# Layer 1 of a two-layer CIN on one Trainium2 core: double batches of leftover products, spread loads, and another order at the beginning

## The chip, the cores and the metric

The kernel runs on one core of one Trainium2 chip. The metric is the device time of one execution in microseconds (us); of several executions the median is taken. The engines are named as the profile names them: PE is TensorE (PEld its weight loads), DVE is VectorE, ACT is ScalarE, POOL is GpSimd, SP is SyncE, whose queue issues most DMAs. A main matmul in fp32 shows as two records in the trace.

## The reference

`x` has 4096 rows, 32 fields and 16 embedding values, in fp32. Two layers of pairwise products follow each other, and their results are summed over the embedding:

```python
def _cin_layer(out, x, W, b, gamma, beta):
    r, _, e = x.shape
    h = jnp.einsum('rne,rfe->rnfe', out, x).reshape(r, -1, e)
    h = jnp.einsum('rce,oc->roe', h, W) + b[None, :, None]
    return _batchnorm(h, gamma, beta)          # over rows and embedding
h1 = _cin_layer(x, x, W1, b1, g1, beta1)       # 32*32 products -> 128 channels
out, direct1 = (h1[:, :64], h1[:, 64:])
direct2 = _cin_layer(out, x, W2, b2, g2, beta2)  # 64*32 products -> 128 channels
agg = jnp.concatenate([direct1, direct2], axis=1)
return agg.sum(axis=-1)
```

Both batchnorms take their mean and variance over all 65536 sites (a site is one row and one embedding value).

## The kernel before

Channels lie on partitions and sites on the free axis, in 128 tiles of 512 sites (`NT`, `T`). The products of layer 1 are symmetric in the two fields, so the two halves of `W1` are added (on POOL, L312), and each pair of fields is multiplied once. For a tile, 512 of the pairs are four blocks of 128 rows: DVE multiplies `a` by `b` (512 KB each, loaded by `load_main` on SP's queue, four buffers each) into `z` in one instruction (L387), and PE does four matmuls of 128 rows into one PSUM bank `ps` (L428). The 16 pairs that are left (fields 16 apart) would fill only 32 partitions with padding, so `r` packs those of eight tiles: 2 groups of 16 rows in each of four row groups. DVE multiplies them into `zr` once in eight tiles (L373), and `add_leftovers` (L380) does four matmuls of 32 rows, each in another row group of the array and for another tile's bank. This is called a batch here. It is issued once in four tiles, ahead of the main matmuls of the tiles that it starts; for tiles 0 to 3 it is issued after tile 1, and it ends the sums of tiles 0 and 1.

The main loop runs over tiles 0 to 123 (L428 in its body). At each turn it issues the loads of the next tile, the product `z`, a batch where one is due, the four main matmuls and `finish(t - 1)`: the eviction of the tile before. An eviction is three activations on ACT (`e` with all channels for the statistics, `kept` for layer 2, `ed` for the direct sum: L352, L355, L358), `bn_stats` on DVE (L115), and for each second tile a store of `kept` and a reduction over the embedding on DVE (L364). PSUM has 8 banks: six in `psum` (tag `ps`) and two in `factors` (tag `f`), which layer 1 does not use but for warming up (`begun`, `BEGIN` matmuls of ones at the start, L239) and for a small product at its end.

Each engine runs its own instructions in the order in which the program names them, but for hints `tc.issue_after`. So what stands ahead of a waiting `z` on DVE, or of a load on SP's queue, is set by where it is written in the loop. `zpool` has four buffers; the second half of the weights (`w1m_sb`) uses one of them at the start. At turn 20 the weights of layer 2 are combined on DVE (`combine_weights`), at turns 12 and 14 two selection matrices are reduced (`spread`, `block`). The list `EARLY` spreads work for layer 2 over the turns: differences of fields of odd tiles (`load_x` into `xs`, `negate`, `difference`, `store_difference`, four times in 24 turns each), and the first operands of layer 2 (`load_b`, `load_bx`, `load_a`).

The last four tiles (124 to 127) are done by halves of the output channels (L461), kept channels first, so that the batchnorm of layer 1 is known while the other halves run. Layer 2 takes 64 steps `c` of two tiles, with four stages `k` each, by a scheme in the manner of Strassen: DVE makes products `zz`, POOL sums of them `t` (L703, L714), PE does the matmuls (L698) in column halves of 64 outputs, two at a time. The products of a stage are issued in four parts, `x2`, `x54` of the stage before (which has waited for POOL), `x31` and `x67`.

At the start SP's queue issues tile 0 in four parts of 256 KB, then `a`, `b` of tile 1, the first `r`, and so on; ACT's queue issues the two halves of the weights of layer 1 (384 KB each) and the batchnorm vectors. The first two tiles' products are made in chunks of 512 columns (`multiply_chunk`, L396).

Of the kernel before, what the change touches and what calls it, by code (L numbers as in the profile page):

```python
# [61 lines left out]
BEGIN = 3  # L63
# [7 lines left out]
def tile_cin(ctx: ExitStack, tc: tile.TileContext, xa, xb, xr, w1, w1m, w2, bn, out):  # L71
# [20 lines left out]

    nc.scalar.activation(const.tile([P, 1], FP, tag="sd", name="table"), eps, AF.Sqrt)
# [93 lines left out]
    def load_x(g, k):  # L187

        at = xb.offset + ((2 * DIFF * g + 1) * WRAP + 2 * k) * T
        nc.sync.dma_start(xs[:, k], bass.AP(xb.tensor, at, [[2 * WRAP * T, DIFF], [4 * T, 8], [1, 2 * T]]))  # L190
# [15 lines left out]
    for g in range(NC // DIFF):  # L206
        at = 14 + 24 * g
        EARLY += [(at + 2 * k, lambda g=g, k=k: load_x(g, k)) for k in range(2)]
        EARLY += [(at + 12 + 2 * k, lambda k=k: negate(k)) for k in range(2)]
        EARLY += [(at + 16 + 2 * k, lambda k=k: difference(k)) for k in range(4)]  # L210
        EARLY += [(at + 23, lambda g=g: store_difference(g))]
    early = []
    EARLY += [(75, lambda: early.append(load_b(0))), (83, lambda: early.append(load_bx(0)))]
    EARLY += [(91 + 8 * k, lambda i=i: early.append(load_a(0, i))) for k, i in enumerate(STAGES)]
# [48 lines left out]
    with ExitStack() as one:  # L263
        lpool = one.enter_context(tc.tile_pool(name="lpool", bufs=4))
# [7 lines left out]
        xs = xpool.tile([P, 2, 2 * T], FP, tag="x", name="xs")  # L272
# [9 lines left out]
        def load_main(t):  # L282
            a = lpool.tile([P, 2 * T], FP, tag="a", name="a")
            b = lpool.tile([P, 2 * T], FP, tag="b", name="b")

            def load(to, part, n):
                at = part * T
                if to is a:
                    at += xa.offset + t * FIELDS * 2 * T
                    source = bass.AP(xa.tensor, at, [[2 * T, FIELDS], [0, 4], [1, n * T]])  # L290
                else:
                    at += xb.offset + (t * WRAP + 2) * T
                    source = bass.AP(xb.tensor, at, [[T, FIELDS], [4 * T, 4], [1, n * T]])
                return nc.sync.dma_start(to[:, part * T : (part + n) * T], source)

            if t == 0:

                parts = ((a, 0, 1), (b, 0, 1), (b, 1, 1), (a, 1, 1))
            else:
                parts = ((a, 0, 2), (b, 0, 2))  # L300
            for part in parts:
                last = load(*part)
            loads.append(last)
            return a, b

        w1_sb = wpool.tile([P, 6, P], FP, tag="w1", name="w1_sb")
        w1m_sb = zpool.tile([P, 6, P], FP, tag="z", name="w1m_sb")
        nc.scalar.dma_start(w1_sb, w1)
        nc.scalar.dma_start(w1m_sb, w1m)

        for k in (slice(0, 1), slice(1, 2), slice(2, 4), slice(4, 6)):
            nc.gpsimd.tensor_tensor(w1_sb[:, k], w1_sb[:, k], w1m_sb[:, k], ALU.add)  # L312
        bn_sb = load_bn()
# [3 lines left out]
        b1, g1, beta1, b2, g2, beta2 = (bn_sb[:, k : k + 1] for k in range(6))  # L317
# [52 lines left out]

        def leftovers(r):
            zr = rpool.tile([P, T], FP, tag="zr", name="zr")
            nc.vector.tensor_tensor(zr, r[:, :T], r[:, T:], ALU.mult)  # L373
            return zr

        def add_leftovers(t, zr, begun=0):

            for k in range(4):
                rows = slice(32 * k, 32 * (k + 1))
                nc.tensor.matmul(  # L380
                    pss[t + k], w1_sb[rows, 4 + t % GROUP // 4, :], zr[rows, :], start=k >= begun, stop=k < begun
                )
# [16 lines left out]
        main = [load_main(t) for t in range(FIRST)]  # L399
        r = load_rem(0)  # L400
        for t in range(NT - ENDING):
            s = t % GROUP
            if s == 4 and t + 4 < NT:
                r = load_rem(t // GROUP + 1)
# [5 lines left out]
            if t < FIRST:  # L410
                for k in range(2):
                    for j in range(2):
                        product = multiply_chunk(z, *main[0], k, j)
            else:

                for k in (slice(0, 1), slice(1, 2)) if t == FIRST else (slice(0, 2),):
                    product = multiply_main(z, *main[0], k)
# [4 lines left out]
            if s % 4 == 0:  # L422
                for k in range(4):
                    pss[t + k] = psum.tile([P, T], FP, tag="ps", name="ps")
            if s % 4 == 0 and t > 0:
                add_leftovers(t, zr)
            for m in range(4):
# [4 lines left out]
                    start=t < FIRST and m == 0,  # L432
                    stop=t >= FIRST and m == 3,
                )
            if t == FIRST - 1:
                add_leftovers(0, zr, FIRST)
            if t > 0 and t < ending - 1:
                evicted = finish(t - 1)
# [5 lines left out]
            if t == 0:  # L444
# [30 lines left out]
        def add_leftovers_halves(banks, zr, direct, begun):  # L475

            for k in range(ENDING):
                rows = slice(32 * k, 32 * (k + 1))
                to = banks[k][half_of[(k + direct) % 2]]
                matmul(to, w1_sb[rows, 5, half_of[direct]], zr[rows, :], k not in begun, k in begun)  # L480

        zs = []
        for k in range(ENDING):
# [3 lines left out]
            queue("dve", lambda: multiply_main(zs[k], *main.pop(0), slice(0, 2)))  # L487

# [367 lines left out]
    for c in range(NC):  # L856
# [3 lines left out]
        for k, i in enumerate(STAGES):  # L860
# [41 lines left out]
            else:  # L902
                stage.x2()
                if waiting:
                    waiting.x54()
                stage.x31()
# [102 lines left out]
```

## Time and profile before

| what | value |
|---|---|
| median of 4 runs (lowest to highest) | 2046.41 us (2046.26 to 2046.56) |
| profiled execution, its span | 2046.56 us, 2044.8 us |
| PE, DVE, POOL, ACT busy (share of the span) | 2028.1 (99%), 1959.4 (96%), 1492.6 (73%), 1186.1 (58%) us |
| main matmuls of layer 1 (L428) | 992 records, 435.9 us busy, mean 597 ns |
| leftover matmuls (L380) | 248 records, 35.4 us busy, mean 640 ns |
| product `z` (L387) | 127 instructions, mean 2270 ns, idle before 43.3 us, 21.4 of it for PE |
| statistics (L115), `e` on ACT (L352) | 124 each, mean 686 and 687 ns |
| first main matmul, first matmul of tile 2 | 8.61, 18.42 us |
| end of layer 1's main loop, layer 2 from | 475.60, 528.60 us |
| DMA | 440.70 MB, mean 216 GB/s; 390 GB/s in the first fortieth |

Records of matmuls overlap: a record is some 0.59 us long, and the next one starts 0.43 us after it. So the busy time of PE is the union of its records, and the pace is read from the starts. Times of one instruction are a mean over its group. "Idle before" is the engine's idle time just ahead of the instruction, with what ended most of it.

### The profile page before, as it was taken

The numbers are of one execution on the slowest core, as the hardware profiler recorded it, in microseconds if no ns is written. First come the engines' busy times: TensorE is split into PE (matmuls) and PEld (weight loads), VectorE is DVE, ScalarE is ACT, GpSimd is POOL, SyncE is SP. The second block draws the span as 40 slices with busy tenths as digits, with TensorE's granted clock in tenths as the row PEclk, the third lists the DMA queues.
The fourth block names the chain that finished last, engine by engine and source line by source line (L and its number), as shares of the span: only waits on it lengthen the run. The fifth ranks groups of instructions, "written<-read, shape, count | busy, mean of one in ns | idle before, by whom it ended". The sixth has DMA issues, their size and how long they took to land.

```text
span 2044.8 us, 24467 instructions
## 1 busy us (share of the span) xinstructions
PE 2028.1 (99%) x8500; PEld 880.6 (43%) x8500; DVE 1959.4 (96%) x1521; ACT 1186.1 (58%) x1914; POOL 1492.6 (73%) x525
## 2 busy tenths in 40 slices
PE   9999999999999999999999999999999999999997
PEld 3444444443344444444444444444444444444443
DVE  8998987998999999999999999999999999999998
ACT  4555554554566666565666555656665565566564
POOL 0000000002999999999999999999999999999996
PEclk9999999999999999999999999999999999999999
DMA  9999999996777777777776767777767777777661
GB/s 390 374 344 368 343 371 342 367 391 188 174 179 180 178 175 173 194 176 179 182 174 167 175 170 180 173 182 176 180 166 174 172 176 180 181 177 175 168 162 42
DMA packets 112380, 440.70 MB, mean 216 GB/s; under 512 B 13056, under 2 KB 13056, under 8 KB 103808
## 3 DMA queue, kind: packets, MB, share of 16 engines
q1 hardware_dynamic: 105840, 418.43, 73.7%
q10 hardware_dynamic: 6416, 20.72, 2.7%
q8 instruction: 66, 1.08, 0.2%
q14 instruction: 58, 0.48, 0.1%
HBM read 417.07 MB, written 22.02 MB: 215 GB/s over the span
## 4 chain that ended last, share of the span: by engine, by line
PE 97%; DVE 1%; DMA 1%; issue 0%; ACT 0%; POOL 0%; DVEq 0%; ACTq 0%; POOLq 0%
PE x L698 73%; PE ps L428 21%; PE ps L380 2%; PE ps L461 1%; DVE zz L667 1%; DMA b<-in_xb 0%; DMA w1m_sb<-in_w1m 0%; DVE zz L672 0%; POOL t L714 0%; ACT f L659 0%; DVE d L934 0%; ACT u L659 0%; DVE both L662 0%; POOL t L703 0%; ACT both L659 0%
## 5 line engine op out<-in xcount | busy, mean ns | idle before, releaser
L714 POOL TENSOR_TENSOR t<-zz,t 128x2048 f32<-128x2048 f32 (+1 forms) x260 | 1168.7, 4496 | 20.7 <-DVE t L662 1.1
L698 PE MATMUL x<-t,s_sb 128*64 128x512 f32 x2040 | 958.3, 592 | 0.4 <-POOL t L714 0.4
L698 PE MATMUL x<-zz,s_sb 128*64 128x512 f32 x2048 | 934.4, 592 | 0.0
L698 PE MATMUL x<-zz,w_sb 128*64 128x512 f32 x2056 | 759.8, 592 | 0.0
L703 POOL TENSOR_TENSOR t<-zz 128x512 f32<-128x512 f32 x255 | 328.5, 1288 | 511.5 <-DVE zz L667 511.4
L667 DVE TENSOR_TENSOR zz<-f,bx 128x2048 f32<-128x2048 f32 x255 | 582.1, 2283 | 19.6 <-ACT f L659 19.6
L659 ACT ACTIVATE f<-a,keep 128x512 f32<-128x512 f32 x512 | 398.2, 778 | 342.6 <-DVE zz L667 304.2
L667 DVE TENSOR_TENSOR zz<-f,b 128x2048 f32<-128x2048 f32 x255 | 582.3, 2283 | 0.1
L698 PEld LDWEIGHTS x<-t,s_sb 128*64 128x64 f32 x2040 | 279.1, 137 | 488.9 <-issue 459.1
L698 PE MATMUL x<-t,w_sb 128*64 128x512 f32 x1020 | 479.3, 592 | 0.0
L428 PE MATMUL ps<-z,w_sb 128*128 128x512 f32 x992 | 435.9, 597 | 2.3 <-POOL w_sb L312 2.3
L698 PEld LDWEIGHTS x<-zz,s_sb 128*64 128x64 f32 x2048 | 279.5, 137 | 249.6 <-issue 241.8
L387 DVE TENSOR_TENSOR z<-a,b 128x2048 f32<-128x2048 f32 (+1 forms) x127 | 288.1, 2270 | 43.3 <-PE ps L428 21.4
L428 PEld LDWEIGHTS ps<-z,w_sb 128*128 128x128 f32 x992 | 186.4, 190 | 249.7 <-issue 229.7
L698 PEld LDWEIGHTS x<-zz,w_sb 128*64 128x64 f32 x2056 | 238.1, 137 | 122.1 <-issue 120.1
L659 ACT ACTIVATE b<-zz 128x512 f32<-128x512 f32 x255 | 152.5, 598 | 187.2 <-DVE zz L667 187.2
L352 ACT ACTIVATE e<-ps,bn_sb 128x512 f32<-128x512 f32 x124 | 85.2, 687 | 215.5 <-PE ps L428 168.4
L662 DVE TENSOR_TENSOR t<-zz,b 128x512 f32<-128x512 f32 x255 | 173.2, 679 | 0.4
L698 PEld LDWEIGHTS x<-t,w_sb 128*64 128x64 f32 x1020 | 139.6, 137 | 0.1
L596 ACT ACTIVATE unread<-e,center 128x512 bf16<-128x512 f32 x122 | 86.2, 707 | 0.0
L358 ACT ACTIVATE ed<-ps,bn_sb 64x512 f32<-64x512 f32 x124 | 84.8, 684 | 2.3
L115 DVE BATCH_NORM_STATS2 stats<-e 128x6 f32<-128x512 f32 x124 | 85.0, 686 | 0.5 <-ACT e L352 0.5
(103 smaller groups left out, 866.9 us busy)
## 6 DMA issues: line engine op xcount, KB each, us to landing
a<-h SPq DMA_DIRECT2D x256, 512.0 KB, 4.6
b<-in_xb SPq DMA_DIRECT2D x64, 1024.0 KB, 9.4
a<-in_xa SPq DMA_DIRECT2D x127, 512.0 KB, 6.9
b<-in_xb SPq DMA_DIRECT2D x127, 512.0 KB, 8.0
bx<-in_xb SPq DMA_DIRECT2D x64, 512.0 KB, 9.3
bx<-x SPq DMA_DIRECT2D x64, 512.0 KB, 10.9
h<-kept ACTq DMA_DIRECT2D x64, 256.0 KB, 5.7
r<-in_xr SPq DMA_DIRECT2D x16, 512.0 KB, 8.4
```

The lines of the kernel that those rows point to most:

```text
L115: nc.vector.bn_stats(self.stats[:, self.at, :], h)
L352: nc.scalar.activation(e, ps, AF.Identity, bias=b1)
L358: done = nc.scalar.activation(ed[to, :], ps[KEEP:, :], AF.Identity, bias=b1[KEEP:])
L387: return nc.vector.tensor_tensor(z[:, k], a.rearrange("p (a t) -> p a t", a=2)[:, k].unsqueeze(2).to_broadcast([P, n, 2, T]), b.rearrange( ...
L428: nc.tensor.matmul(pss[t], w1_sb[:, m, :], z[:, m // 2, m % 2, :], start=t < FIRST and m == 0, stop=t >= FIRST and m == 3,)
L596: return nc.scalar.activation(unread, e[:, s], AF.Square, bias=center[:, s], accum_out=squares[:, s, c : c + 1])
L659: return queue("act", lambda: nc.scalar.activation(to, source, AF.Identity, **scale_bias))
L662: return dve(lambda: nc.vector.tensor_tensor(to, x, y, ALU.add))
L667: dve(lambda: nc.vector.tensor_tensor(z, a, b.rearrange("p (k q) t -> p k q t", k=2), ALU.mult))
L698: queue("pe", lambda: nc.tensor.matmul(self.of[x], w, b, start=start, stop=stop))
L703: queue("pool", lambda: nc.gpsimd.tensor_tensor(t2[:, 0], z[:, 1, 0], z[:, 0, 0], ALU.add))
L714: queue("pool", lambda: nc.gpsimd.tensor_tensor(t14[:, k, q], z[:, 2 + k.start : 2 + k.stop, q], twice[:, k, q], ALU.subtract))
```

## The change

*Batches.* From tile 8 on, eight leftover matmuls are issued at once, at tiles 8, 16 ... 120: four for tiles t-4 to t-1, whose sums they end, and four for tiles t to t+3, whose sums they begin. One batch of four is left at the end of tile 1, and the batch of the ending. `r` is packed with a shift of four tiles for that, in 17 groups instead of 16, and one more `zr` is made in the ending. Tiles hold their bank longer, so layer 1 uses all 8 banks, and `finish` follows four turns later than the tile (`finish(t - 4)`), with a catch-up in the last turns.

*Loads.* The fields for the differences come from an array of their own, packed on the host, in which each load is contiguous for a partition; these loads come at turns 8 and 11 (and 24 later each time) instead of 14 and 16, and those of layer 2's first operands at 65, 73 and 88 to 112 instead of 75, 83 and 91 to 115. `a` and `b` have five buffers instead of four. `r` is loaded at turns 3, 9, 17 ... instead of 4, 12, 20 ...

*Beginning.* `b` of tile 0 is issued on ACT's queue and `a` of tile 0 on SP's, each whole; then on SP's queue both halves of the main weights in one load (512 KB), `a` and `b` of tile 1, the leftover weights (256 KB), `r`, and the tiles in order. The first slice of the weights is added on DVE after the first chunk of `z`, the others on POOL. `BEGIN` is 4, and the activation that brings in the table of the square root comes after the first loads.

*Layer 2.* In the stages with k > 0, `x31` is issued ahead of the `x54` of the stage before.

```diff
 DIFF = 16
-BEGIN = 3
+BEGIN = 4
...
-    nc.scalar.activation(const.tile([P, 1], FP, tag="sd", name="table"), eps, AF.Sqrt)
...
-        at = xb.offset + ((2 * DIFF * g + 1) * WRAP + 2 * k) * T
-        nc.sync.dma_start(xs[:, k], bass.AP(xb.tensor, at, [[2 * WRAP * T, DIFF], [4 * T, 8], [1, 2 * T]]))
+        nc.sync.dma_start(xs[:, k], xd_in[2 * g + k])
...
     for g in range(NC // DIFF):
-        at = 14 + 24 * g
-        EARLY += [(at + 2 * k, lambda g=g, k=k: load_x(g, k)) for k in range(2)]
+        at = 8 + 24 * g
+        EARLY += [(at + 3 * k, lambda g=g, k=k: load_x(g, k)) for k in range(2)]
         EARLY += [(at + 12 + 2 * k, lambda k=k: negate(k)) for k in range(2)]
...
     early = []
-    EARLY += [(75, lambda: early.append(load_b(0))), (83, lambda: early.append(load_bx(0)))]
-    EARLY += [(91 + 8 * k, lambda i=i: early.append(load_a(0, i))) for k, i in enumerate(STAGES)]
+    EARLY += [(65, lambda: early.append(load_b(0))), (73, lambda: early.append(load_bx(0)))]
+    EARLY += [(88 + 8 * k, lambda i=i: early.append(load_a(0, i))) for k, i in enumerate(STAGES)]
     loads = []
...
     with ExitStack() as one:
-        lpool = one.enter_context(tc.tile_pool(name="lpool", bufs=4))
+        lpool = one.enter_context(tc.tile_pool(name="lpool", bufs=5))
         rpool = one.enter_context(tc.tile_pool(name="rpool", bufs=1))
...
-        xs = xpool.tile([P, 2, 2 * T], FP, tag="x", name="xs")
+        xs = bpool.tile([P, 2, 2 * T], FP, tag="bx", name="xs")
         xd = xpool.tile([P, 2 * T], FP, tag="xd", name="xd")
...
-            def load(to, part, n):
-                at = part * T
-                if to is a:
-                    at += xa.offset + t * FIELDS * 2 * T
-                    source = bass.AP(xa.tensor, at, [[2 * T, FIELDS], [0, 4], [1, n * T]])
-                else:
-                    at += xb.offset + (t * WRAP + 2) * T
-                    source = bass.AP(xb.tensor, at, [[T, FIELDS], [4 * T, 4], [1, n * T]])
-                return nc.sync.dma_start(to[:, part * T : (part + n) * T], source)
-            if t == 0:
-                parts = ((a, 0, 1), (b, 0, 1), (b, 1, 1), (a, 1, 1))
-            else:
-                parts = ((a, 0, 2), (b, 0, 2))
-            for part in parts:
-                last = load(*part)
-            loads.append(last)
+            nc.sync.dma_start(
+                a, bass.AP(xa.tensor, xa.offset + t * FIELDS * 2 * T, [[2 * T, FIELDS], [0, 4], [1, 2 * T]])
+            )
+            at_b = bass.AP(xb.tensor, xb.offset + (t * WRAP + 2) * T, [[T, FIELDS], [4 * T, 4], [1, 2 * T]])
+            loads.append((nc.sync if t > 0 else nc.scalar).dma_start(b, at_b))
             return a, b
         w1_sb = wpool.tile([P, 6, P], FP, tag="w1", name="w1_sb")
-        w1m_sb = zpool.tile([P, 6, P], FP, tag="z", name="w1m_sb")
-        nc.scalar.dma_start(w1_sb, w1)
-        nc.scalar.dma_start(w1m_sb, w1m)
-        for k in (slice(0, 1), slice(1, 2), slice(2, 4), slice(4, 6)):
-            nc.gpsimd.tensor_tensor(w1_sb[:, k], w1_sb[:, k], w1m_sb[:, k], ALU.add)
-        bn_sb = load_bn()
+        w1_both = zpool.tile([P, 2, 4, P], FP, tag="z", name="w1_both")
+        left_both = zpool.tile([P, 2, 2, P], FP, tag="z", name="left_both")
         w2_sb = const.tile([P, 16, P], FP, tag="w2", name="w2_sb")
...
         neg_sb = const.tile([P, 2, 2, KEEP], FP, tag="neg", name="neg_sb")
-        b1, g1, beta1, b2, g2, beta2 = (bn_sb[:, k : k + 1] for k in range(6))
...
+        def multiply_leftovers(zr, r):
+            return nc.vector.tensor_tensor(zr, r[:, :T], r[:, T:], ALU.mult)
...
             zr = rpool.tile([P, T], FP, tag="zr", name="zr")
-            nc.vector.tensor_tensor(zr, r[:, :T], r[:, T:], ALU.mult)
+            multiply_leftovers(zr, r)
             return zr
-        def add_leftovers(t, zr, begun=0):
+        def bank(t):
+            pool, tag = (psum, "ps") if t % GROUP < 6 else (factors, "f")
+            return pool.tile([P, T], FP, tag=tag, name="ps")
+        def ends_with_leftovers(t):
+            return t % GROUP >= 4 or t < FIRST
+        def add_leftovers(t, zr):
...
                 rows = slice(32 * k, 32 * (k + 1))
-                nc.tensor.matmul(
-                    pss[t + k], w1_sb[rows, 4 + t % GROUP // 4, :], zr[rows, :], start=k >= begun, stop=k < begun
-                )
+                last = ends_with_leftovers(t + k)
+                w = w1_sb[rows, 4 + (t + 4) % GROUP // 4, :]
+                nc.tensor.matmul(pss[t + k], w, zr[rows, :], start=not last, stop=last)
...
         ending = NT - ENDING
-        main = [load_main(t) for t in range(FIRST)]
+        main = [load_main(0)]
+        nc.sync.dma_start(w1_both, w1)
+        bn_sb = load_bn()
+        b1, g1, beta1, b2, g2, beta2 = (bn_sb[:, k : k + 1] for k in range(6))
+        nc.scalar.activation(const.tile([P, 1], FP, tag="sd", name="table"), eps, AF.Sqrt)
+        main += [load_main(t) for t in range(1, FIRST)]
+        nc.sync.dma_start(left_both, w1_left)
+        for k in (slice(1, 2), slice(2, 4)):
+            nc.gpsimd.tensor_tensor(w1_sb[:, k], w1_both[:, 0, k], w1_both[:, 1, k], ALU.add)
+        nc.gpsimd.tensor_tensor(w1_sb[:, 4:], left_both[:, 0], left_both[:, 1], ALU.add)
         r = load_rem(0)
...
             s = t % GROUP
-            if s == 4 and t + 4 < NT:
+            if s == 1 and t > 1 or t == 3:
...
                         product = multiply_chunk(z, *main[0], k, j)
+                        if t == k == j == 0:
+                            with tc.issue_after(product.ins):
+                                nc.vector.tensor_tensor(w1_sb[:, 0], w1_both[:, 0, 0], w1_both[:, 1, 0], ALU.add)
             else:
...
                 for k in range(4):
-                    pss[t + k] = psum.tile([P, T], FP, tag="ps", name="ps")
-            if s % 4 == 0 and t > 0:
+                    pss[t + k] = bank(t + k)
+            if s == 0 and t > 0:
+                add_leftovers(t - 4, zr)
                 add_leftovers(t, zr)
...
                     z[:, m // 2, m % 2, :],
-                    start=t < FIRST and m == 0,
-                    stop=t >= FIRST and m == 3,
+                    start=ends_with_leftovers(t) and m == 0,
+                    stop=not ends_with_leftovers(t) and m == 3,
                 )
             if t == FIRST - 1:
-                add_leftovers(0, zr, FIRST)
-            if t > 0 and t < ending - 1:
-                evicted = finish(t - 1)
+                add_leftovers(0, zr)
+            if t >= ending - 2:
+                evicted = finish(t - 2)
+            elif t >= ending - 4:
+                for done in range(2 * t - ending, 2 * t - ending + 2):
+                    evicted = finish(done)
+            elif t >= 4:
+                evicted = finish(t - 4)
             if t == 20:
...
                     nc.scalar.activation(b1_swapped[x], b1[y], AF.Identity)
-            if t == 0:
+            if t < 4:
                 continue
...
                 to = banks[k][half_of[(k + direct) % 2]]
-                matmul(to, w1_sb[rows, 5, half_of[direct]], zr[rows, :], k not in begun, k in begun)
+                matmul(to, w1_sb[rows, 4, half_of[direct]], zr[rows, :], k not in begun, k in begun)
...
             queue("dve", lambda: multiply_main(zs[k], *main.pop(0), slice(0, 2)))
+            if k == 0:
+                zr = rpool.tile([P, T], FP, tag="zr", name="zr")
+                queue("dve", lambda: multiply_leftovers(zr, r))
...
+                products = [stage.x31]
                 if waiting:
-                    waiting.x54()
-                stage.x31()
+                    products.insert(k > 0, waiting.x54)
+                for issue in products:
+                    issue()
                 stage.x67()
...
     xb = xt[:, np.arange(WRAP) % FIELDS]
-    xr = np.stack([xt[:, :16], xt[:, 16:]], axis=2).reshape(NT // GROUP, GROUP // 4, 4, 16, 2, T)
-    xr = xr.transpose(0, 2, 1, 3, 4, 5).reshape(NT // GROUP, P, 2, T)
+    xr = np.stack([xt[:, :16], xt[:, 16:]], axis=2)
+    xr = np.concatenate([xr[:4], xr, xr[-4:]]).reshape(NT // GROUP + 1, GROUP // 4, 4, 16, 2, T)
+    xr = xr.transpose(0, 2, 1, 3, 4, 5).reshape(NT // GROUP + 1, P, 2, T)
+    xd = xt[1::2].reshape(NC // DIFF, DIFF, 8, 2, 2, T).transpose(0, 3, 1, 2, 4, 5).reshape(-1, P, 2 * T)
...
             w1m[32 * q + 16 * u + lo, 4 + u] = w1nf[:, lo + 16, lo].T
+    w1_both = np.stack([w1t, w1m], axis=1)
     w2t = np.ascontiguousarray(w2.reshape(P, 4, 16, 8, 4).transpose(2, 3, 1, 4, 0)).reshape(P, 16, P)
...
     arrays, args = {}, []
-    for name, a in (("xa", xa), ("xb", xb), ("xr", xr), ("w1", w1t), ("w1m", w1m), ("w2", w2t), ("bn", bn)):
+    for name, a in (("xa", xa), ("xb", xb), ("xr", xr), ("xd", xd), ("w1", w1_both[:, :, :4]), ("left", w1_both[:, :, 4:]), ("w2", w2t), ("bn", bn)):
         a = np.ascontiguousarray(a)
```

## The prediction

> **What bounds the kernel now.** I read the page's first part and the chain first. TensorE (PE) is busy for 99% of the span and it is nearly the whole chain, so only what shortens PE's own row of work, or a wait in it, moves the end.
>
> ```profile
> PE 2028.1 (99%) x8500; PEld 880.6 (43%) x8500; DVE 1959.4 (96%) x1521; ACT 1186.1 (58%) x1914; POOL 1492.6 (73%) x525
> PE x L698 73%; PE ps L428 21%; PE ps L380 2%; PE ps L461 1%; DVE zz L667 1%; DMA b<-in_xb 0%; DMA w1m_sb<-in_w1m 0%; DVE zz L672 0%; POOL t L714 0%; ACT f L659 0%; DVE d L934 0%; ACT u L659 0%; DVE both L662 0%; POOL t L703 0%; ACT both L659 0%
> ```
>
> The chain in order of time (start, length, what) shows where that row can give. In layer 1 it repeats exactly: 13.93 us of main matmuls, then a leftover batch, every 15.003 us (26.62 to 41.62). Nothing waits from 18.42 to the end of layer 1.
>
> ```profile
> 8.61 8.80 PE ps L428 x16
> 18.49 7.06 PE ps L428 x16
> 26.62 13.93 PE ps L428 x32
> 41.62 13.93 PE ps L428 x32
> 528.60 1498.59 PE x L698 x6980
> ```
>
> The timeline of PE and of its weight loads around one leftover batch gives the price of a batch. Columns: start, busy, engine, line, operation, count, idle before.
>
> ```profile
> 40.48 1.14 PE L380 MATMUL ps<-zr,w_sb 32*128 32x512 f32 x8
> 41.55 2.84 PE L428 MATMUL ps<-z,w_sb 128*128 128x512 f32 x6
> 40.48 0.31 PEld L380 LDWEIGHTS ps<-zr,w_sb 32*128 32x128 f32 x8 [0.76 <-issue]
> 41.55 0.30 PEld L428 LDWEIGHTS ps<-z,w_sb 128*128 128x128 f32 x2 [0.76 <-issue]
> 42.09 0.19 PEld L428 LDWEIGHTS ps<-z,w_sb 128*128 128x128 f32 x1 [0.24 <-issue]
> ```
>
> Main records start 0.429 us apart: 8 to a tile, 3.433 us. Four tiles make 13.73, so a batch costs 15.003 - 13.73 = 1.27. Its four matmuls of 32 rows start within 7 ns of each other and are two rows of records, 0.858. The other 0.41 is four gaps of about 0.1 us: into the batch, between its two rows, out of it, and between the first two main records after it. The weight loads show why: at those places they wait 0.76 us instead of 0.24, so they are not hidden.
>
> The start is the other place. The waits and the timeline of DVE (z products) and PE:
>
> ```profile
> 1.55 4.80 PE L239 MATMUL begun<-ones 128*128 128x512 f32 x6 [1.55 <-DVE ones L236]
> 8.61 8.80 PE L428 MATMUL ps<-z,w_sb 128*128 128x512 f32 x16 [2.26 <-POOL w_sb L312]
> 18.42 1.98 PE L428 MATMUL ps<-z,w_sb 128*128 128x512 f32 x4
> 7.76 6.25 DVE L396 TENSOR_TENSOR z<-a,b 128x512 f32<-128x512 f32 x8 [6.12 <-DMA b<-in_xb]
> 15.33 4.76 DVE L387 TENSOR_TENSOR z<-a,b 128x1024 f32<-128x1024 f32 x3 [0.72 <-DMA b<-in_xb]
> ```
>
> PE starts at 8.61 and reaches tile 2 at 18.42. The windows of the same stretch (us, busy of PE, PEld, DVE, ACT, POOL, granted clock, DMA share, GB/s):
>
> ```profile
> 5.50:9.00 3.50, 1.24 (x3) 0.30 (x2) 1.24 (x2) 0.79 (x4) 1.90 (x3) 0.99 1.03 389
> 9.00:12.40 3.40, 3.40 (x5) 1.29 (x4) 3.27 (x5) 0.21 (x2) 1.23 (x2) 0.51 1.03 423
> 12.40:30.00 17.60, 17.60 (x52) 7.11 (x51) 16.26 (x15) 7.76 (x12) 0.00 (x0) 1.00 1.03 423
> ```
>
> DMA is full from 5.5 on: one 512 KB load lands every 1.25 us, whatever queue it was issued on.
>
> **Term 1, the batches.** After, one batch of four stays at the end of tile 1 and 15 batches of eight come at tiles 8, 16 ... 120; before there were 31 batches of four. Rows of real work stay the same, 15 excursions go. If the second set of four follows the first as main records follow each other, a double batch is 1.27 + 0.858 = 2.13 against 2.54, a gain of 0.41; 15 of them are **6.15**. If each change of weights by row groups costs its 0.1 gap, the second set brings two more gaps and only 0.2 is saved, 3.0 in all. The trace has no two such sets in a row. I take 6.15: the pairs of column halves in layer 2, where every pair changes its weights, run without gaps (6980 records, two at a time, in 1498.59: 0.429 a pair), and the 0.1 stands just as well between two plain main records after a batch, so it goes with the change of shape, not with the set. The Trainium skill, "TensorEngine Tiling (Array Packing)", Key Properties, says that a change of tiling mode drains the engine, but not whether sets of one mode follow without a gap; by it alone the sum would be the same 6.15.
>
> **Term 2, the start.** Before, 4.27 MB had to land until b of tile 2 (15.24); after, it is about as much, but in another order. a and b of tile 0 go out together on SP's and ACT's queues; Before, 384 KB had landed by 4.04 and 1.5 MB by 8.32, so 1 MB lies between 5.6 and 7.1 at 1.25 per 512 KB; I put both operands at 6.6, towards the end that the start showed. At that pace the main weights (512 KB) follow at 7.85, b of tile 1 at 10.35, the leftover weights (256 KB) and r at 12.25, b of tile 2 at 14.75 (15.24 by equal bytes). DVE adds the first slice, and the first matmul starts near 8.1. POOL's adds of slices 1 (0.45) and 2 to 3 (1.17) start at 7.85 and keep ahead of PE. Two tiles of 3.43 and a batch end at 8.1 + 6.87 + 1.1 = 16.1, and half of z of tile 2 takes 1.17 after its b, so 15.95 (16.4). Tile 2 begins at 16.1 instead of 18.42: **2.3**. Part of this is the clock: before, the window 9.0 to 12.4 ran at 0.51, after a window in which PE was busy 1.24 of 3.5 us. A fourth warm-up matmul and the earlier start raise that to about 70%, and I take the full clock. If half a clock is granted all the same, half of a 3.4 window is lost, 1.7.
>
> The Trainium skill, "DMA: Bandwidth & Descriptors", Issuing engines are not separate DMA queues, says that the queues of SP and ACT feed the same engines and that two of them save only issue time. That speaks against the two queues as such; the 1.03 share agrees. By it the two operands would still come before the weights, and only about 0.7 (one issue, the second 0.6 to 0.7 us after the first) would be won by the second queue.
>
> After that the loads bind: r of the second group now comes before the operands of tile 4, whose b lands at 21.0 instead of 20.22; z of tile 4 is ready at 23.3, PE wants it at 22.97: **-0.35**.
>
> **Term 3, a new wait.** The first double batch starts at T = 37.1. Tiles 4 to 7 all end with it, so their evictions start together: ACT needs 1.98 a tile (0.59, 0.68, 0.71), the first starts T + 1.15, and e of tile 7 ends at T + 7.8. In DVE's program the statistics of tiles 4 to 7, a reduction and the next leftover product stand ahead of z of tile 10. So this z starts at T + 8.4 and ends at T + 10.7 (2.27), but PE wants it at T + 2.13 + 6.87 = T + 9.0: **-1.7**. z of tile 13 comes after one more reduction of 0.95 (spread): **-0.35**. By tile 16 DVE has got ahead; from tile 32 the four z of a cycle stand ahead of the statistics, and the nearest z is done 4.3 us early. Before, the early z were 0.7 to 3.3 us ahead. The two waits cannot be below nothing together, since a z that is early saves PE nothing; at most I allow 2.9 (one more statistics and reduction, 1.2, in front of tile 13).
>
> **What costs nothing.** The extra leftover product in the ending (0.67 on DVE) lies in a stretch with DVE busy 13 of 15 us. Packed loads for the differences, their new places and the fifth buffer pair: DMA share stays near 0.99, but z has more cover than before; bank by bank, evictions end 9.3 and 17.9 us after a batch starts, before the bank is wanted. In layer 2 the products x31 come ahead of the waiting x54: they need zz 1.7 us earlier. It ends 0.68 us after the stage's start in the tightest early stage and is wanted at 0.86; later it is 2.5 to 3.7 us ahead of the start. That 0.18 us hides it; without it the early stages would pay tenths. The 0.62 us pause at 528.0 waits for POOL and stays.
>
> **Sum:** 6.15 + 2.3 - 0.35 - 1.7 - 0.35 = 6.05. The profiled execution took 2046.56 (span 2044.8 and 1.76 around it), 0.15 above the median of 2046.41. 2046.56 - 6.05 = 2040.5.
>
> **Rivals.** *Each set pays its gaps:* gain 3.0 - 0.1 = 2.9, so 2043.6; for it, the gap between the two rows inside a batch; against it, that the same gap follows between main records. *The start gives nothing back:* half clock (-1.7) or loads later by as much: 4.0 to 4.3, so 2042.4; for it, DMA is full. *No early wait:* ACT or DVE is ahead of what I read: 8.1, so 2038.5. *Slower:* the wait of term 3 comes back at every double batch, since all four evictions behind a batch hold DVE. It decides from 0.41 a cycle on; at 1.7 in each of the 14 later cycles it costs 24, so 2064. For it, DVE is busy 30.0 of 30 us from 30 to 60; against it, DVE is busy only 360 of 400 us from 60 to 460, and the program's order changes. *Nothing changes* would need the batches to have been hidden, and the chain has them.
>
> **How the numbers follow.** Forecast 0.58, paying gaps 0.12, no gain at the start 0.10, no early wait 0.11, slower 0.09. The range goes from no early wait with loads 0.9 sooner (2037.6; 1.0 is the early bound above) to paying gaps (2043.8). A measurement of this kernel can tell about 0.2%, 4.1 us. The forecast, no early wait, and a third of the case at the start are faster by more: 0.72; the rest of that and paying gaps are within it: 0.19; slower 0.09.
>
> **What would show it.** Right: main tiles in steps of 8 with a period of 29.6; 16 records of a double batch within 2.1 us, and only one long wait of the weight loads ahead of it; first matmul near 8.1 and tile 2 near 16.1 at clock 1.0; a PE wait for z of about 1.7 near 46 us and no such wait after 70. Wrong: gaps of 0.1 between the sets, a window at half clock before 16, waits of PE for z at each cycle, or waits at the stages of layer 2.

## The result: 3.9 us less, two thirds of the forecast

The changed kernel takes 2042.54 us (median of 33 executions, 2042.01 to 2043.48), the one before 2046.40 (53 executions, 2045.01 to 2048.12). The ratio is 0.9982 (0.9977 to 0.9987). The time lies inside the range, but 2.0 us above the forecast of 2040.5. The interval of the ratio does not reach 1, so the gain is clear of the noise; but the prediction gave a chance of 0.72 to a gain of more than 0.2% (4.1 us), and at 3.9 us it is just less. The profiled execution took 2042.22 (span 2040.5).

The page, its busy times and its chain by line:

```profile
PE 2023.5 (99%) x8502; PEld 880.5 (43%) x8502; DVE 1957.1 (96%) x1523; ACT 1190.0 (58%) x1914; POOL 1491.1 (73%) x524
PE x L714 75%; PE ps L435 20%; PE ps L373 1%; PE ps L474 1%; DVE z L378 0%; DMA w_both<-in_w 0%; POOL t L730 0%; DVE zz L683 0%; ACT e L333 0%; ACT ed L339 0%; ACT kept L336 0%; DVE d L953 0%; ACT u L675 0%; POOL t L719 0%; ACT both L675 0%
```

PE is still the chain, but pieces of DVE's `z` have come into it. In order of time (start, length, what):

```profile
7.92 2.05 PE ps L435 x4
...
17.81 2.27 DVE z L378
21.87 2.21 DVE z L378
24.13 14.00 PE ps L435 x32
...
46.50 2.29 DVE z L378
48.83 10.57 PE ps L435 x24
...
71.89 27.66 PE ps L435 x64
99.55 1.93 PE ps L373 x16
101.48 27.66 PE ps L435 x64
```

From 71.89 on eight tiles and a double batch repeat every 29.59 us (30.00 before). Before that the chain holds three `z`: PE waits a little at tiles 3 and 4 (20 to 24), and 1.7 us at tile 10 (48.83); 0.26 more follows at tiles 13 and 14. DVE's timeline shows what stood ahead of the `z` of tile 4 (21.79) and of tile 10 (46.50):

```profile
20.00 0.69 DVE L114 BATCH_NORM_STATS2 stats<-e 128x6 f32<-128x512 f32 x1
20.60 0.67 DVE L345 TENSOR_REDUCE d<-ed 128x32 f32<-128x512 f32 x1
21.19 0.68 DVE L353 TENSOR_TENSOR zr<-r 128x512 f32<-128x512 f32 x1
21.79 2.28 DVE L378 TENSOR_TENSOR z<-a,b 128x2048 f32<-128x2048 f32 x1
...
39.94 0.69 DVE L114 BATCH_NORM_STATS2 stats<-e 128x6 f32<-128x512 f32 x1 [2.29 <-ACT e L333]
...
45.89 0.69 DVE L114 BATCH_NORM_STATS2 stats<-e 128x6 f32<-128x512 f32 x1 [0.69 <-ACT e L333]
46.50 2.27 DVE L378 TENSOR_TENSOR z<-a,b 128x2048 f32<-128x2048 f32 x1
```

The clock at the start, in the windows of the prediction, was full:

```profile
5.50:9.00 3.50, 2.61 (x7) 0.84 (x6) 2.12 (x4) 1.01 (x5) 1.38 (x2) 1.00 1.02 409
9.00:12.40 3.40, 3.37 (x9) 1.34 (x9) 3.40 (x5) 0.00 (x0) 1.23 (x2) 1.00 1.04 419
```

A double batch, in the timeline of PE and of its weight loads:

```profile
69.89 2.00 PE L373 MATMUL ps<-zr,w_sb 32*128 32x512 f32 x16
69.89 0.31 PEld L373 LDWEIGHTS ps<-zr,w_sb 32*128 32x128 f32 x8 [0.76 <-issue]
70.43 0.20 PEld L373 LDWEIGHTS ps<-zr,w_sb 32*128 32x128 f32 x4 [0.22 <-issue]
70.86 0.20 PEld L373 LDWEIGHTS ps<-zr,w_sb 32*128 32x128 f32 x4 [0.23 <-issue]
71.82 0.30 PEld L435 LDWEIGHTS ps<-z,w_sb 128*128 128x128 f32 x2 [0.76 <-issue]
```

The unhidden loads (0.76) stand at the entry and at the exit; inside, the second set loads in 0.22, like any matmul.

The profiled gain of 4.3 us adds up so (tile starts from the trace's records of PE): tile 2 starts at 16.39 instead of 18.42, +2.03; 15 excursions fewer (an excursion is the change of PE to matmuls of 32 rows and back), +6.15; waits for `z`, each with the 0.1 by which the record after it comes late, at tiles 3 and 4, -0.87, at tile 10, -1.98, at tiles 13 and 14, -0.26; the ending, from its first leftover to layer 2's first product, 17.33 instead of 16.38, -0.95; layer 2 from first to last product 1539.82 in both; after it 0.2 less, +0.2. The sum is 4.3, as the spans have it.

### The profile page after: what moved, and what is told of

It reads as the page before. It is cut to its first block, busy times and chain, and to the rows that moved or that the text cites. A ratio compares the mean times of both kernels' runs of the same rounds, so it can differ in the third digit from the quotient of the medians.

```text
span 2040.5 us, 24501 instructions
## 1 busy us (share of the span) xinstructions
PE 2023.5 (99%) x8502; PEld 880.5 (43%) x8502; DVE 1957.1 (96%) x1523; ACT 1190.0 (58%) x1914; POOL 1491.1 (73%) x524
## 4 chain that ended last, share of the span: by engine, by line
PE 97%; DVE 1%; ACT 0%; issue 0%; DMA 0%; POOL 0%; DVEq 0%; SPq 0%; ACTq 0%; POOLq 0%
PE x L714 75%; PE ps L435 20%; PE ps L373 1%; PE ps L474 1%; DVE z L378 0%; DMA w_both<-in_w 0%; POOL t L730 0%; DVE zz L683 0%; ACT e L333 0%; ACT ed L339 0%; ACT kept L336 0%; DVE d L953 0%; ACT u L675 0%; POOL t L719 0%; ACT both L675 0%
## 5 line engine op out<-in xcount | busy, mean ns | idle before, releaser
L714 PE MATMUL x<-zz,s_sb 128*64 128x512 f32 x2048 | 955.4, 592 | 0.0
L714 PE MATMUL x<-t,s_sb 128*64 128x512 f32 x2040 | 927.4, 592 | 0.2 <-POOL t L730 0.2
L714 PE MATMUL x<-zz,w_sb 128*64 128x512 f32 x2056 | 728.8, 592 | 0.0
```

Of the source, the lines that this page charges most:

```text
L714: queue("pe", lambda: nc.tensor.matmul(self.of[x], w, b, start=start, stop=stop))
```

## The experiments

Spans are of the one profiled execution, medians of 10 or 11 executions unless a number stands by. Executions of one kernel differ by over 1 us, and the kernel before had medians of 2045.8 to 2046.5 in the four sessions (on three chips), so the tile starts in the profiles carry the argument and the medians confirm it.

**One excursion more at each double batch.**

```diff
                 add_leftovers(t - 4, zr)
-                add_leftovers(t, zr)
             for m in range(4):
+                if s == 0 and t > 0 and m == 1:
+                    add_leftovers(t, zr, 1)
```

> The changed kernel, but at tiles 8, 16 ... 120 the second four leftover matmuls come after the first main matmul of the tile instead of directly after the first four. The rows of work are the same; only the number of excursions to matmuls of 32 rows rises from 16 to 31. Theory (an excursion costs about 0.41 us in four gaps around it, and a set that follows another pays none): the period of eight tiles goes from 29.59 back to 30.00 us, and the span from 2040.5 to about 2046.3 (15 x 0.41 = 6.2 more, less a few tenths of the early wait for z). Rival (each change of weights by row groups pays its gaps, whether sets are neighbours or not): about 3 us more. Rival (the batches were never on the path): no change.

Span 2045.3, median 2047.07. The period of eight tiles is 30.00 us. PE's timeline:

```profile
69.38 1.14 PE L373 MATMUL ps<-zr,w_sb 32*128 32x512 f32 x8
70.45 1.12 PE L436 MATMUL ps<-z,w_sb 128*128 128x512 f32 x2
71.50 1.14 PE L373 MATMUL ps<-zr,w_sb 32*128 32x512 f32 x8
```

Up by 4.8 in the span and 4.5 in the median: 6.15, less 1.8 of the wait of tile 10, which has nearly gone because PE comes later (tile 10 follows tile 9 after 3.52), plus 0.6 more wait at tile 13; tile 2 came 0.26 later in this execution, and the ending took 0.42 less. The excursion is what costs, not the set.

**VectorE's order before tile 10.**

```diff
+            elif t == GROUP + 3:
+                with tc.issue_after(product.ins):
+                    for done in range(4, GROUP):
+                        evicted = finish(done)
-            elif t >= 4:
+            elif t >= 4 and not GROUP <= t < GROUP + 3:
                 evicted = finish(t - 4)
```

> The changed kernel, but the evictions of tiles 4 to 7 are written after the product z of tile 11, so that on VectorE the products of tiles 8 to 11 stand ahead of the statistics of tiles 4 to 7; everything else is the same. Theory (the wait of TensorE for z before tile 10 is a matter of VectorE's order): the wait of 1.7 us near 47 us is gone, tile 16 starts about 2 us sooner, and the span falls from 2040.5 to about 2038.4. Rival (the loads of tiles 9 to 11 came late): the wait stays, at the same tile, and VectorE waits for a DMA instead of for ScalarE; span 2040.5. Rival (VectorE has no room to catch up, the wait only moves to a later tile): span 2039.5 to 2040.5 with new waits between tiles 12 and 16.

Span 2038.8, median 2041.35. DVE's waits from 36 to 62 us, first of the changed kernel, then here (what waited, us in total, times, longest):

```profile
DVE stats L114 <- ACT e L333: 3.0, 2, 2.3
```

```profile
DVE z L378 <- DMA b<-in_xb: 1.8, 2, 1.3
DVE zr L353 <- DMA r<-in_xr: 0.7, 1, 0.7
```

Tiles 9, 10 and 11 now start 3.44 us apart. With DVE free, loads are the next to be late, but PE does not feel them there; 0.5 of the wait moves to tile 14. So the wait was a matter of order, as term 3 had it, and 1.7 of it comes back.

**The ending.**

```diff
-            if t >= ending - 2:
+            if t == ending - 2:
                 evicted = finish(t - 2)
+            elif t == ending - 1:
+                pass
 ...
-            for t in (ending - 2, ending - 1):
+            for t in (ending - 3, ending - 2, ending - 1):
```

> The changed kernel, but the eviction of tile 121 is written after the last product z, so that one statistics and one reduction (1.2 us) on VectorE stand behind the products of tiles 126 and 127 instead of ahead of them. Theory (0.95 us was lost in the ending because z of tile 127 came 0.4 us late, and the column halves of tiles 126 and 127 then ran unpaired): the pairs of the ending run 0.429 us apart without a gap again, and the span falls by 0.95 to about 2039.5. Rival (the gaps in the ending come from the banks or from ScalarE, which evicts later than before): the gaps stay. Rival (the gain is given back, since layer 2's first products wait for the kept channels' statistics): the ending is shorter, but layer 2 starts as late as now, span 2040.5.

Span 2039.9, median 2042.03 (one execution at 2045.13). In the changed kernel the weight loads of the ending show the wait:

```profile
474.11 0.14 PEld L474 LDWEIGHTS ps<-z,w_sb 128*64 128x64 f32 x2 [0.28 <-issue]
474.54 0.14 PEld L474 LDWEIGHTS ps<-z,w_sb 128*64 128x64 f32 x1 [0.28 <-issue]
474.97 0.14 PEld L474 LDWEIGHTS ps<-z,w_sb 128*64 128x64 f32 x1 [0.29 <-issue]
475.87 0.20 PEld L474 LDWEIGHTS ps<-z,w_sb 128*64 128x64 f32 x4 [0.77 <-DVE z L378]
```

Column halves run in pairs, so loads come by twos; at 474.54 and 474.97 one comes alone, for tile 126, and the loads for tile 127 begin at 475.87. In this run that wait is gone and the pairs start 0.429 apart up to 7.51 us into the ending. But another has come: the halves behind them wait twice for ACT's kept channels of the same bank, since ACT's eviction of tile 123 now waits 5.7 us for the statistics that were put behind the products, and the kept channels come after it. The ending takes 16.89: half of the 0.95 is back. Where of the two only the reduction is moved (0.6 us on DVE; the last two kernels below, which change other places too) it is 16.73.

**The old beginning.**

```diff
-BEGIN = 4
+BEGIN = 3
 ...
-        main = [load_main(0)]
-        nc.sync.dma_start(w1_both, w1)
+        nc.scalar.dma_start(w1_sb, w1)
+        nc.scalar.dma_start(w1m_sb, w1_left)
 ...
+        main = [load_main(t) for t in range(FIRST)]
```

> The changed kernel with the beginning of the kernel before: four parts of tile 0 on SP's queue, the two halves of the weights on ACT's queue, all additions of weights on POOL, three warm-up matmuls, the table activation first. Theory (the new beginning is worth the 2.0 us by which tile 2 starts sooner): tile 2 starts near 18.4 us instead of 16.4, and the span rises by 1.5 to 2.0, to 2042.0 to 2042.5; less than the 2.0 if the early waits for z shrink with a later start. Rival (the start is hidden, the wait before tile 10 swallows it): span within 0.3 of 2040.5.

A miss: span 2039.3, below the changed kernel; median 2042.12 (2041.07 to 2042.44). Tile 2 starts at 16.83, not 18.4, with the clock full in this execution. Its eleven times split by the mean granted clock that is listed with each: five at 0.998 lie at 2041.07 to 2041.82, six at 0.997 at 2042.12 to 2042.44. And there is no wait before tile 10 (tile 9 at 43.65, tile 10 at 47.08): with the old beginning DVE makes `z` of tile 9 right behind that of tile 8, from 35.38 to 39.86, ahead of the statistics of tiles 4 to 7; in the changed kernel it comes at 40.55, behind the first of them, which waited 2.29 us for ACT.

**Four kernels on the start**, in one session. First, `b` of tile 0 on SP's queue:

```diff
-            loads.append((nc.sync if t > 0 else nc.scalar).dma_start(b, at_b))
+            loads.append(nc.sync.dma_start(b, at_b))
```

> The changed kernel, but b of tile 0 is issued on SP's queue after a, as all others, not on ACT's. Theory (both queues feed the same engines; the loads are bound by bytes): b of tile 0 lands at 6.2 to 6.9 us instead of 6.21, the weights still near 7.6, later loads where they are; the first matmul moves by 0.3 at most, tile 2 by at most 0.2, and the span stays within 0.3 of 2040.5. Rival (a second queue moves more bytes in the first 5 us): all loads land 0.7 to 1 us later, tile 2 starts near 17.2 us, span up by 0.5 to 1.

A miss the other way: median 2043.58, span 2041.9. By the trace, `b` of tile 0 lands at 6.64 (6.21), the weights at 8.79 (7.55), `b` of tile 2 at 15.69 (14.40); tile 2 starts at 17.64. The rival was right, and by more than it said: from 5.0 to 6.5 us the DMA engines are busy 0.84 with one queue (276 GB/s) and 1.02 with two (364 GB/s). The second queue is worth 1.0 us.

Second and third, the warm-up: `BEGIN = 3` in the changed kernel, and `BEGIN = 4` in the kernel before.

> The changed kernel with three warm-up matmuls instead of four. The granted clock changes in steps of 3.41 us whose place against the start differs from run to run (5.15, 5.98, 6.74 and 6.96 us in four profiles so far). Theory (a window in which TensorE is busy for about a third is followed by one at half clock, which costs 1 to 1.7 us; the fourth warm-up matmul keeps it away): the times split into those as now, 2042.0 to 2043, and some about 1 us longer; a profile of such a run has a stretch at 0.5 between 8.5 and 12.5 us. Rival (the early first matmul at 7.9 us suffices without it): as now, median 2042.5, no stretch at 0.5.

> The kernel before, with four warm-up matmuls instead of three and nothing else. Its executions so far form two clusters, 2045.0 to 2045.5 and 2046.1 to 2047.1, and the profiled one, of the upper cluster, has a stretch at half clock from 8.94 to 12.36 us. Theory (most of the 2.0 us by which the changed kernel reaches tile 2 sooner is the clock): tile 2 starts near 17 us instead of 18.42, no stretch at 0.5, nearly all times lie in the lower cluster, median 2045.2. Rival (the clusters have another cause, and the sooner tile 2 is owed to the order of the loads): both clusters stay, and tile 2 at the same clock stays near 18.4.

The changed kernel hardly needs the fourth matmul: 2042.53, nine of eleven times at 2042.2 to 2043.4, two at 2043.6 and 2043.8. The kernel before does: 2045.30 instead of 2046.54, ten of eleven times at most 2045.72, tile 2 at 17.04. The windows of this kernel (columns as in the prediction):

```profile
5.50:9.00 3.50, 3.15 (x6) 0.96 (x4) 1.51 (x2) 1.01 (x5) 2.17 (x4) 1.00 1.02 391
9.00:12.40 3.40, 3.29 (x8) 1.16 (x7) 3.27 (x5) 0.00 (x0) 0.95 (x1) 1.00 1.03 420
```

PE busy 3.15 instead of 1.24 us, and then clock 1.00 instead of 0.51. Ten of its eleven executions have a mean clock of 0.998; of 32 executions of the kernel before, taken along with it, ten have it (2044.97 to 2045.60), and 22 have less (2046.12 to 2048.41). So 1.2 us of the whole gain is the full clock at the start. One warm-up matmul gives it to the kernel before as well; the changed kernel has it nearly always with three.

Fourth, the changed kernel with the old beginning and four warm-ups (the diff above without `BEGIN`):

> The changed kernel with the beginning of the kernel before, but with four warm-up matmuls. With three of them the times went from 2041.07 to 2042.44, and the profiled one, 2041.07, had the full clock, tile 2 at 16.83 us and no wait for z before tile 10. Theory (the order of loads and weights at the beginning is worth 0.4 us until tile 2 and loses more by the order that it leaves on VectorE; the rest was the clock): nearly all times at 2041.0 to 2041.4, 1.3 below the changed kernel, with tile 2 at 16.8. Rival (the lower times with the old beginning were chance): median as with three, 2042.1, or above.

Median 2041.52 (2040.97 to 2042.20), span 2039.2, tile 2 at 16.76: the changed kernel is 1.0 slower than its own batches and loads behind the old beginning. The new beginning wins 0.4 until tile 2; it loses 2.0 before tile 10 and 0.3 more than the old one at tiles 3 and 4, and the old one loses 0.6 more at tiles 13 and 14.

**Batches and loads apart.** The old beginning with four warm-ups in all of them. Double batches alone (the packing and the turns of layer 2's first operands go back too, not shown):

```diff
-        at = 8 + 24 * g
-        EARLY += [(at + 3 * k, lambda g=g, k=k: load_x(g, k)) for k in range(2)]
+        at = 14 + 24 * g
+        EARLY += [(at + 2 * k, lambda g=g, k=k: load_x(g, k)) for k in range(2)]
 ...
-        lpool = one.enter_context(tc.tile_pool(name="lpool", bufs=5))
+        lpool = one.enter_context(tc.tile_pool(name="lpool", bufs=4))
 ...
-                    products.insert(k > 0, waiting.x54)
+                    products.insert(0, waiting.x54)
```

> The kernel with the old beginning and four warm-up matmuls, and in addition the old loads (four buffer pairs, differences not packed, old turns) and the old order of layer 2's products: of the change only the double batches are left. Theory (loads and order of layer 2 have cover and are worth nothing): span within 0.3 of the 2039.25 that the kernel with the new loads and order had, median 2041.5, no waits of TensorE in layer 2 beyond those near 535 us. Rival (the spread loads keep products from coming late): waits of TensorE for z between 40 and 110 us, span up by 1 or more. Rival (the order in layer 2 moves its few waits): a change of 0.2 to 0.6 near 530 us, of either sign.

The rival was right: median 2049.20 (2045.33 to 2051.76), slower than before. PE's waits from 320 to 365 us, and then the windows of this kernel and of the one with the new loads:

```profile
PE ps L443 <- DVE z L399: 5.9, 2, 3.8
```

```profile
330.00:357.00 27.00, 21.08 (x60) 8.33 (x58) 17.38 (x16) 10.79 (x17) 0.00 (x0) 0.98 1.01 345
357.00:363.00 6.00, 6.00 (x8) 2.48 (x9) 6.00 (x6) 4.72 (x8) 0.00 (x0) 0.51 0.88 292
```

```profile
330.00:357.00 27.00, 27.00 (x75) 11.66 (x74) 23.56 (x21) 16.77 (x26) 0.00 (x0) 1.00 0.95 358
357.00:363.00 6.00, 6.00 (x15) 2.66 (x14) 6.00 (x5) 0.00 (x0) 0.00 (x0) 1.00 1.02 414
```

Around tile 90 the first operands of layer 2 and the loads for the differences come together; the share of DMA is 1.01, and DVE waits 9.3 us for `b` in 320 to 365. Single batches bore that: in the kernel before DVE waited 11.3 us there, and PE not at all. With double batches DVE needs products ahead when the statistics of four tiles come at once, and it had none: the product for tile 91 ended as tile 91 began, and then statistics, reductions and a leftover product held the next one until 354.54. Waits of 2.15 and 3.77 us come of it, and with the second a stretch of 6.83 us at half clock. Layer 2 takes 1539.80 us in both: the order of its products is worth nothing. The loads alone, on the kernel before:

> The kernel before with four warm-up matmuls, and of the change only the loads: packed differences, new turns, five buffer pairs. With the old loads and single batches there was no wait of TensorE for a load after 18 us, and the median was 2045.3; with double batches and the old loads there were waits of 2.3 and 3.9 us near 346 and 357 us and a stretch at half clock behind them, median 2049.2. Theory (the loads are worth nothing by themselves and 7 to 8 us under double batches, which ask for bank and product in bursts): median 2045.3, span within 0.3 of 2043.4, no waits in layer 1. Rival (the loads gain by themselves): below 2044.5. Rival (they cost something with single batches, since they come sooner): waits for z before 110 us, above 2045.8.

Median 2045.10, span 2043.3. So, in medians: single batches with old loads 2045.3, with new loads 2045.1; double batches with old loads 2049.2, with new loads 2041.5. Which part of the new loads is the cover (the packing, the places or the fifth buffer pair) is not shown, since they were taken back together.

**Relief for VectorE.** With the old beginning and four warm-ups, and with the new beginning:

```diff
-            if t == 20:
-                combine_weights()
+            if t == 44:
+                with tc.issue_after(product.ins):
+                    combine_weights()
 ...
+            elif 4 <= t < 6:
+                if t == 4:
+                    product4 = product
+                with tc.issue_after(product4.ins):
+                    evicted = finish(t - 4)
 ...
-                evicted = finish(t - 2)
+                evicted = finish(t - 2, t - 2 != ending - 3)
 ...
+            sum_direct((ending - 3) // 2)
```

> The changed kernel with the old beginning and four warm-up matmuls, and VectorE relieved in three places: statistics of tiles 0 and 1 and the second leftover product after the product of tile 4; the combination of layer 2's weights (2.9 us) at turn 44, spread and block (1.6 us) at turns 46 and 48; the reduction of tiles 120 and 121 after the last product z. Theory (all that is left beyond the row of TensorE's work is VectorE's order): no wait for z at tiles 4 and 13 (0.45 and 0.87 now), the ending in 16.4 us instead of 17.3; span 2039.25 - 2.2 = 2037.0, median 2039.3. Rival (loads bind next): waits for z stay in part, with VectorE waiting for a DMA; span 2038 to 2039.

> The changed kernel, its own beginning kept, with the same three reliefs of VectorE and the statistics of tiles 4 to 7 after the product of tile 11. Theory: the waits for z at tiles 3, 4, 10 and 13 (0.2, 0.55, 2.0, 0.3) and the 0.95 of the ending go; span 2040.5 - 4.0 = 2036.5, median 2038.6, so the new beginning is worth its 0.4 us against the old one once VectorE's order is right. Rival (loads bind next, since the new beginning has the same bytes ahead of tile 2): waits at tiles 3 to 13 stay in part, span 2037.5 to 2039, no better than with the old beginning.

With the old beginning: median 2039.27 of 5 (2039.11 to 2039.65), ratio to before 0.9966 (0.9953 to 0.9979), the best of all and 3.3 below the changed kernel. After tile 2 no wait of PE for `z` is left in layer 1. Its span, 2037.9, is 0.9 above what was expected: 0.6 stands at tile 2 (17.38 instead of 16.76), since the loads landed later in that execution (first matmul at 8.96 instead of 8.07), and 0.3 in the ending (16.73, where 16.4 was expected). With the new beginning: 2040.20 of 6, span 2038.3; one long wait is left, and DVE's timeline names it:

```profile
22.35 2.29 DVE L378 TENSOR_TENSOR z<-a,b 128x2048 f32<-128x2048 f32 x1 [2.69 <-DMA b<-in_xb]
```

`b` of tile 4 landed at 22.23 (20.90 in the changed kernel), and tile 4 starts 1.5 late. So, relieved, the new beginning was bound by loads in this execution, as the rival said, and it is no better than the old one. How much of the 1.3 by which this `b` landed later is chance is open.

## Why the forecast was partly right

*Term 1, right.* 6.15 forecast, 6.15 found, period 29.59. That sets of one shape follow without a gap is shown by the loads inside the batch, and that the excursion costs 0.41 by undoing it. The rival of paying gaps fell.

*Term 2, near in size, its parts not told apart.* Tile 2 came 2.03 sooner for 2.3 forecast; the first matmul came at 7.92 (8.1 forecast), but tile 0 took 3.87 instead of 3.43. The prediction named the clock as a part without a size, and it is the larger one: only 0.65 remains against the kernel before with four warm-ups (17.04). And the clock of the one profiled execution was taken for the kernel's: the 53 times of the kernel before lie at 2045.75 and below or at 2046.09 and above, and 36 of them, two thirds, in the upper cluster, that of the half-clock stretch. That the profiled execution came from the cluster in which the median lies too was luck. The weighing of the queues failed too. The Trainium skill, "DMA: Bandwidth & Descriptors", Issuing engines are not separate DMA queues, says that a second queue saves only issue time. Here one queue made the weights land 1.2 later and the kernel 1.0 slower, where the issue is 0.7; the measurement decides.

*The loads of tile 4, wrong cause.* -0.35 was put on `b` of tile 4. It landed at 20.90 as forecast (21.0), but `z` began at 21.79, behind a statistics, a reduction and a leftover product on DVE; with tile 3 it came to -0.87.

*Term 3, right.* -1.7 and -0.35 forecast, -1.98 and -0.26 found; moving the statistics took it away. It did not return at later cycles, so the slower case fell.

*What costs nothing, wrong twice.* The ending was covered by an average: DVE busy 13 of 15 us. What counted was the margin of the last product, and it was gone: `z` of tile 127 ended at 475.82, while its partner, tile 126, had begun at 474.97. Two records then ran alone there and two more at the end (481.94 and 482.36); two lengths of a record and a gap of 0.1 are the 0.95. That the reduction ahead of it on DVE had a share is shown by moving it (0.6 back); that the leftover product had one is argued. And the loads were put at nothing beside double batches: they gain nothing alone (0.2 in the medians), but they are the cover without which double batches lose 3.9 instead of gaining 3.8. The prediction did not ask what its first term would be without them.

By terms, the 2.0 us between forecast and median are 0.95 for the ending, 0.5 for tiles 3 and 4, 0.3 each for tile 2 and tile 10, less 0.1 at tiles 13 and 14 and 0.2 after layer 2; 0.3 is the difference of the profiled execution from the median.

## What to carry to other kernels

A batch that is made larger to save changeovers makes the work behind it come in bursts: look for the queue that holds that work, and for what stands behind it there, at the beginning and at the end of the loop, where the steady margin is not yet or no longer built up. A load or a step that is worth nothing alone can be the cover of another part of the change, so cost each part with and without the others. And before a stretch at half clock in one profile is booked as a term, look at the spread of all times: two clusters 1.2 us apart say that it is there in some executions only.

## What the runs showed of the hardware

The steps of the granted clock are 3.41 us long (3.413 in the trace), and their place against the start varied from 4.42 to 7.70 us in the profiles. The Trainium skill, "TensorE: Matmul & The Clock Gate", What's actually happening, says that this window runs freely and does not reset with the kernel; the profiles agree. A stretch in which PE was busy 1.24 of 3.5 us was followed by one at half clock; with 1.70 us in 5.7 to 9.1 (old beginning, three warm-ups) the clock stayed full. In the kernel of double batches alone one pause of 3.77 us came with 6.83 us at half clock, which lose 3.4 more, so that wait was charged almost twice.

Two column halves that lost step did not make it up by themselves: in the changed kernel's ending one half ran two records alone (474.97 and 475.39), then both went on in pairs, and before the next batch of 32 rows the other half ran its last two (481.94 and 482.36) by itself.
